# Two-layer spectral convolution on one core: x loaded first, bytes and loads moved at three stage starts, the first mixing weights on another engine

## The chip, the cores and the metric

One core of one Trainium2 chip. The metric is the device time of one execution in microseconds; a profiled execution also gives a span, from the first to the last instruction. Engines: TensorE (PE, with its weight loads shown as PEld), VectorE (DVE), ScalarE (ACT), GpSimd (POOL) and SyncE (SP). SP computes nothing here; its queue (SPq) issues nearly all transfers, one after the other.

## The reference, cut to what matters

The input x is 16 images of 16 channels of 256 x 256 values, float32. Layer 0 normalises x by groups of two channels, applies a circular 3 x 3 convolution (written with FFTs) and adds x. Layer 1 normalises again, goes to the frequency domain, mixes channels at each frequency with a matrix built from poles and residues, goes back, and adds a transient term:

```
x = x + conv3x3(gn(x), weight)
alpha = fft2(gn(x))
A = 1/(i*w1 - pole1);  Bm = 1/(i*w2 - pole2)
S = einsum('ikpq,oikp,xikq->oxik', residue, A, Bm)
r1 = einsum('biox,oxik->bkox', alpha, S)
r2 = einsum('bikpq,ikpq->bkpq', einsum(alpha, A, Bm), residue)
x = x + real(ifft2(r1)) + real(sum of r2 * exp(pole1*ty) * exp(pole2*tx)) / (Nx*Ny)
```

## The kernel before

The work is one program in four stages, one after the other. Each stage opens its own pools in the on-chip memory, over the bytes of the stage before. A tile that lands on bytes of an earlier tile waits until that tile's last readers and writers are done; the kernel inserts these waits by itself. Inside the stages the order on each engine is the order in which the code records it (`manual_schedule`), and every engine and queue works in order. So an instruction that waits holds up all that stand behind it on its engine. Transfers use eight DMA semaphores in turn: the issue of a transfer waits until the one eight places earlier has landed.

**Stage 1, convolution (lines 100 to 651).** An image is held as two halves of 128 partitions x 18 x 258, loaded by `load_x` (line 111). Per image `x_stats` takes 16 `bn_stats` of VectorE (line 156), eight from each half, aggregates them (line 164), spreads the groups' sums over the partitions with small matmuls (line 168), and folds the scale into the convolution's weights (`conv_weights`). `sum_taps` (line 136) reads the weights' tile `wband` and is run between the eighth and the ninth `bn_stats` of image 0. Then `conv(g)` gives TensorE its matmuls (line 239); ScalarE evicts them to a tile `vt` with sums (lines 256, 264; four buffers), VectorE adds and subtracts the mirrored rows (lines 221, 222), and the two results, `vsum` and `vt`, are stored to the scratch `vD` (line 282). For the first image nothing is there to overlap with: the convolution starts when its statistics are done. Between the convolution's steps, tables for the later stages are made from the poles: exponentials, the table `cD` of residues over frequencies, and others, which need the reciprocal step sizes `rd` (lines 74 to 76).

Before stage 1, `const` (line 47) loads `cols`, `kmask` and `fold2`, then `step` (the first two values of ty and tx, from which `rd` is made) and a part of `tabE` and `tabO`: seven loads ahead of x.

**Stage 2, transform (lines 654 to 851).** 64 units, each of one channel and four images. `load_v` (line 684) reads `vD` into a tile `s` with four transfers, two units ahead; `fold` (line 692) makes `vq` from it on VectorE and GpSimd; `lines` (lines 720, 728, 736) transforms along y and scales on ScalarE; `columns` (lines 748 to 783) transforms along x into `spec`, and after the fourth unit of a channel `spec` (4 MB) is stored to `aD` (line 848). `spec` alternates between two places, one for even and one for odd channels. `first_slots` (line 792) multiplies by `sgn`, a column of -1 and a column of 1, set by two memsets at the start of the stage (lines 680, 681). `sgn` is a tile of 4 KB per partition, of which 8 bytes are used; it also keeps the two places of `spec` apart. The first three units' loads are issued by GpSimd (line 815).

**Stage 3, mixing (lines 855 to 1109).** `ct` (4 MB) is read from `cD` (line 885). `weights(g)` (line 904) builds one group's factors `v` on VectorE and multiplies them by four column masks, `m4`, into the tile `w` of 2048 columns on GpSimd (line 933). `sums` (line 962) multiplies `ct` and `w` on TensorE into the mixing matrices, which are evicted to `sg`; `mix` (line 1028) applies them to `abd`, the spectra loaded from `aD` (line 1014) into tiles that GpSimd first clears (line 977). The first `sums` need `weights(0)`, and after eight rounds `weights(32)`. `ct` lies over the bytes of the even `spec` and, with its last 96 bytes, over the first bytes of `sgn`'s tile.

**Stage 4, inverse transform (lines 1112 to 1306).** Back along x and y, the transient term added, the residual from `vD` added, and the result stored. The change does not touch it.

Of the kernel before, what the change touches and what calls it, by code (L numbers as in the profile page):

```python
# [9 lines left out]
FP = mybir.dt.float32  # L10
AF = mybir.ActivationFunctionType
ALU = mybir.AluOpType
# [5 lines left out]
C = 16  # L18
N = 256
P = 128  # L20
# [4 lines left out]
def conv_then_laplace_kernel(ctx: ExitStack, tc: tile.TileContext, a: dict, out: bass.AP):  # L25
# [15 lines left out]
    nc = tc.nc  # L41
    x = a["x"]
# [1 line left out]
    cp = ctx.enter_context(tc.tile_pool(name="const", bufs=1))  # L44
    dp = ctx.enter_context(tc.tile_pool(name="scratch", bufs=1, space=DRAM))

    def const(name, shape, src=None):
        t = cp.tile(shape, FP, name=name, tag=name)
        nc.sync.dma_start(out=t, in_=a[name] if src is None else src)
        return t  # L50

    cols = const("cols", [P, 24])
# [15 lines left out]
        nc.vector.tensor_scalar(o, k, d, 2.0 * PI, ALU.mult, ALU.mult)  # L68

    step = cp.tile([P, 2, 2], FP, name="step", tag="step")  # L70
    nc.sync.dma_start(out=step[:, 0], in_=a["ty"][:, 0:2].to_broadcast([P, 2]))
    nc.sync.dma_start(out=step[:, 1], in_=a["tx"][:, 0:2].to_broadcast([P, 2]))
    rd = cp.tile([P, 2], FP, name="rd", tag="rd")
    nc.vector.tensor_tensor(rd, step[:, :, 1], step[:, :, 0], ALU.subtract)
    nc.vector.tensor_scalar(rd, rd, float(N), None, ALU.mult)
    nc.vector.reciprocal(rd, rd)

    ptab = ExitStack()
    tp = ptab.enter_context(tc.tile_pool(name="tables", bufs=1))
# [4 lines left out]
    tabO = tp.tile([P, C + 1, P], FP, name="tabO", tag="tabO")  # L84
    hB = tp.tile([P, 2, C, P], FP, name="hB", tag="hB")
    coef = [tp.tile([P, C, 4, 4, 2], FP, name=f"coef{j}", tag=f"coef{j}") for j in range(2)]
    nc.sync.dma_start(out=tabE[:, 0], in_=a["trig"][:, 0])
    nc.sync.dma_start(out=tabO[:, C], in_=a["trig"][:, 1])

# [8 lines left out]
    p1 = ExitStack()  # L98
# [9 lines left out]
    psu = p1.enter_context(tc.tile_pool(name="p_setup", bufs=1, space=PSUM))  # L108
    p1.enter_context(tc.manual_schedule())

    def load_x(b, h):
        t = xp.tile([P, 18, N + 2], FP, name="xt", tag="xt")
        nc.sync.dma_start(out=t, in_=x[b][:, 16 * h : 16 * h + 18])
        return t

    halves = {0: [load_x(0, 0)]}

    def load1(name, shape, pool=wp):
        t = pool.tile(shape, FP, name=name, tag=name)
# [4 lines left out]
    imask = load1("imask", [P, 2, 3, 32], tp)  # L124
    g128 = load1("g128", [P, P], tp)
    m16 = load1("m16", [P, C], tp)
    halves[0].append(load_x(0, 1))
    halves[1] = [load_x(1, h) for h in range(2)]
    nc.sync.dma_start(out=jmat, in_=a["jmat"])
    ones = tp.tile([P, P], FP, name="ones", tag="ones")  # L130
# [487 lines left out]
    for j, (_, piece) in enumerate(x_stats(0)):  # L618
        if j == 8:
            sum_taps()  # L620
        piece()

    at_step = {}
# [37 lines left out]
    def pool(stage, name, bufs=1, **kw):  # L661
        return stage.enter_context(tc.tile_pool(name=name, bufs=bufs, reuse_waits="tile", **kw))
# [3 lines left out]
    fp = pool(p1, "fold_2", 2)  # L666
    lp = pool(p1, "lines", 2)
    a0 = pool(p1, "spec_even")
    kp = pool(p1, "b_const")
    a1 = pool(p1, "spec_odd")  # L670
    kpp = pool(p1, "sines", 3)
    prp = pool(p1, "prod", 2)
    pa = pool(p1, "p_y", 3, space=PSUM)
    px = pool(p1, "p_x", 4, space=PSUM)
    pd = pool(p1, "p_d", space=PSUM)
    p1.enter_context(tc.manual_schedule())


    sgn = kp.tile([P, 1024], FP, name="sgn", tag="sgn")[:, 0:2]
    nc.vector.memset(sgn[:, 0:1], -1.0)  # L680
    nc.vector.memset(sgn[:, 1:2], 1.0)
    m, n = cols[:, 16:17], cols[:, 17:18]

    def load_v(i, b0, eng=nc.sync):
# [127 lines left out]

    units = [(i, b0) for i in range(C) for b0 in range(0, B, 4)]

    loaded = {u: load_v(*units[u], nc.gpsimd) for u in range(3)}
    vq = fold(*units[0], loaded.pop(0))
    nc.vector.bn_aggr(ms[:, B - 1], vst[:, B - 1])
    rest = v_stats(B - 4, B, lambda: pa.tile([P, 512], FP, name="ps_y", tag="ps_y"))
    last = None
# [84 lines left out]
    def weights(g):  # L904

        shape = [P, 32, 4]
        u = up.tile([P, 4, 32, 4], FP, name="u", tag="u")
        w, den, e, f = (u[:, j] for j in range(4))  # L910
        pr2, pre, pim = (prU[:, j].unsqueeze(2).to_broadcast(shape) for j in range(3))
        nc.vector.tensor_tensor(
            w,
            omg[:, g].unsqueeze(1).to_broadcast(shape),
            pims.unsqueeze(2).to_broadcast(shape),
            ALU.subtract,
        )
        nc.vector.tensor_tensor(den, w, w, ALU.mult)
        nc.vector.tensor_tensor(den, den, pr2, ALU.add)
# [10 lines left out]
        nc.vector.tensor_scalar(v[:, :, 0, 1], v[:, :, 1, 0], -1.0, None, ALU.mult)  # L930
        wt = wp.tile([P, 4, 8, 2, 32], FP, name="w", tag="w")
        full = [P, 64, 4, 8]
        nc.gpsimd.tensor_tensor(  # L933
            wt.rearrange("p a k o (i m) -> p (a k o) i m", i=4),
            v.rearrange("p a o r s -> p (a o) (r s)").unsqueeze(2).to_broadcast(full),
            m4.unsqueeze(1).unsqueeze(3).to_broadcast(full),
            ALU.mult,
        )
        return wt
# [516 lines left out]
```

## Time and profile before

Median of three runs 2817.53 us (2812.63 to 2821.07); the profiled execution has a span of 2806.7 us. Stages by the first and last matmuls of each, from the busy times by stretch:

| stretch, us | what | PE busy | DVE | ACT | POOL | PE clock | DMA share |
|---|---|---|---|---|---|---|---|
| 0 to 29.5 | ahead of the convolution | 1.70 | 13.89 | 1.49 | 0.19 | 1.00 | 0.87 |
| 29.5 to 643.0 | convolution | 526.45 | 518.62 | 435.03 | 279.73 | 0.95 | 0.74 |
| 643.0 to 655.8 | between | 0.03 | 5.75 | 2.96 | 0.00 | 0.52 | 0.61 |
| 655.8 to 1276.6 | transform | 617.85 | 520.81 | 371.65 | 220.00 | 0.99 | 0.58 |
| 1276.6 to 1300.7 | between | 0.01 | 16.82 | 0.58 | 14.16 | 0.61 | 0.85 |
| 1300.7 to 2010.0 | mixing | 705.02 | 340.95 | 378.11 | 122.44 | 0.99 | 0.67 |
| 2010.0 to 2806.7 | inverse transform | 765.72 | 511.49 | 332.94 | 439.03 | 0.99 | 0.86 |

Busy is in us; the clock is the share of full speed that TensorE was granted, and the DMA share is the mean busy share of the core's 16 DMA engines. A profile line of the timeline gives start, duration, engine, source line, operation, output and inputs; a bracket at its end is the idle time of that engine before it and what seems to have ended it. The releaser is inferred, and where several things are waited for only one is named.

### The profile page before, as it was taken

What the parts mean: (1) busy time and instruction counts of PE and PEld (TensorE: products, weight loads), DVE (VectorE), ACT (ScalarE), POOL (GpSimd) and SP (SyncE); (2) the same over time, 40 slices, a digit from 0 to 9 for tenths busy, and PEclk for the clock granted to TensorE, in tenths of its full rate; (3) what the DMA queues carried; (4) which work ended last, traced back from release to release, by engine and by line L of the source; (5) the groups of instructions that cost most, each with busy time, mean ns of one, the idle gap of its engine ahead of it and who ended that gap; (6) DMA issues with size and microseconds to landing.
All of it is one profiled execution on the core that took longest, in us unless ns stands there. A gap on an engine that the chain in (4) does not pass through costs nothing.

```text
span 2806.7 us, 93073 instructions
## 1 busy us (share of the span) xinstructions
PE 2616.8 (93%) x39600; PEld 1958.4 (70%) x39600; DVE 1928.3 (69%) x3562; ACT 1522.8 (54%) x3090; POOL 1075.6 (38%) x997
## 2 busy tenths in 40 slices
PE   5878988797999999996999999999989999999998
PEld 2434444355777777774888888888778888888887
DVE  6888998867888888885454444444346666666666
ACT  3767777664666666663455555555434444444443
POOL 1543466513333333334111111111165656565653
PEclk9999999898999999998999999999999999999999
DMA  7776887655665656654766666676688999989995
GB/s 270 255 248 247 286 285 267 230 185 166 229 229 208 213 203 240 227 193 162 200 189 194 190 192 192 194 195 193 198 274 284 289 284 288 283 286 286 288 284 179
DMA packets 479375, 652.82 MB, mean 233 GB/s; under 512 B 51352, under 2 KB 457880, under 8 KB 465008
## 3 DMA queue, kind: packets, MB, share of 16 engines
q1 hardware_dynamic: 477248, 637.56, 70.5%
q8 instruction: 312, 5.11, 0.7%
q0 software_dynamic: 1568, 5.11, 0.6%
q10 hardware_dynamic: 144, 4.19, 0.3%
q14 instruction: 103, 0.84, 0.1%
HBM read 367.22 MB, written 279.50 MB: 230 GB/s over the span
## 4 chain that ended last, share of the span: by engine, by line
PE 61%; DVE 14%; DMA 12%; POOL 4%; issue 4%; SPq 2%; ACT 1%; DVEq 0%; POOLq 0%; ACTq 0%
PE ps_mix L1028 16%; PE ps_s L962 9%; PE ps_y L720 8%; PE ps_y L728 8%; DMA yk<-yD 6%; PE ps_x L763 4%; PE ps_conv L239 4%; PE ps_p L1212 3%; DVE r L1245 3%; PE ps_f L1236 3%; PE ps_f L1237 3%; DMA out_y<-ol 3%; DVE xst L156 2%; DMA xt<-in_x 2%; SPq L1159 2%
## 5 line engine op out<-in xcount | busy, mean ns | idle before, releaser
L1028 PEld LDWEIGHTS ps_mix<-abd,sg 128*64 128x64 f32 x8192 | 449.1, 138 | 61.5 <-ACT sg L1085 48.9
L1028 PE MATMUL ps_mix<-abd,sg 128*64 128x128 f32 x8192 | 480.0, 276 | 9.5 <-ACT yt L1090 9.5
L239 PE MATMUL ps_conv<-xt,wc 32*32 32x512 f32 x12288 | 463.3, 618 | 27.2 <-issue 24.8
L1176 POOL TENSOR_TENSOR u<-yk 128x512 f32<-128x512 f32 (+1 forms) x268 | 346.0, 1322 | 317.7 <-PE ps_p L1212 210.3
L736 ACT ACTIVATE t<-ps_y,vmr 128x384 f32<-128x384 f32 x512 | 297.2, 581 | 166.7 <-PE ps_y L728 166.6
L239 PEld LDWEIGHTS ps_conv<-xt,wc 32*32 32x32 f32 x12288 | 231.4, 105 | 214.4 <-issue 139.4
L933 POOL TENSOR_TENSOR w<-v,mcol 128x2048 f32<-128x2048 f32 x33 | 119.3, 3616 | 575.3 <-DVE v L930 546.9
L1090 DVE COPY yt<-ps_mix 128x512 f32<-128x512 f32 x128 | 88.5, 691 | 360.7 <-PE ps_mix L1028 238.5
L720 PE MATMUL ps_y<-tabE,vq 128*128 128x256 f32 x1024 | 313.5, 388 | 15.0 <-DVE vq L709 13.4
L728 PE MATMUL ps_y<-tabO,vq 128*128 128x256 f32 x1024 | 306.1, 381 | 0.0
L1236 PE MATMUL ps_f<-pt,inv 128*128 128x256 f32 x1008 | 300.4, 380 | 0.0
L1090 ACT COPY yt<-ps_mix 128x512 f32<-128x512 f32 x384 | 220.5, 586 | 146.5 <-PE ps_mix L1028 88.4
L1237 PE MATMUL ps_f<-hs,ey 128*128 128x256 f32 x1008 | 299.8, 379 | 0.0
L1212 PEld LDWEIGHTS ps_p<-inv,u 128*128 128x128 f32 x2048 | 266.0, 193 | 45.0 <-issue 25.1
L1212 PE MATMUL ps_p<-inv,u 128*128 128x128 f32 x2048 | 279.4, 280 | 8.4 <-POOL u L1180 8.3
L962 PE MATMUL ps_s<-ct,w 64*32 64x256 f32 x8448 | 261.2, 382 | 24.4 <-POOL abd L977 24.1
L1240 DVE TENSOR_TENSOR r<-ps_f,q 128x256 f32<-128x256 f32 x256 | 106.9, 418 | 251.5 <-ACT q L1239 251.5
L1085 ACT COPY sg<-ps_s 128x512 f32<-128x512 f32 x248 | 159.7, 645 | 190.7 <-PE ps_s L962 190.6
L720 PEld LDWEIGHTS ps_y<-tabE,vq 128*128 128x128 f32 x1024 | 189.7, 191 | 91.5 <-ACT q L776 50.3
L256 ACT ACTIVATE vt<-ps_conv,xq 128x512 f32<-128x512 f32 x256 | 167.0, 680 | 155.9 <-PE ps_conv L239 140.7
L1239 ACT COPY q<-ps_f 128x256 f32<-128x256 f32 x256 | 95.4, 372 | 287.6 <-PE ps_f L1237 284.4
L1214 ACT COPY pt<-ps_p 128x512 f32<-128x512 f32 x256 | 150.1, 586 | 133.3 <-PE ps_p L1212 117.9
(238 smaller groups left out, 4170.4 us busy)
## 6 DMA issues: line engine op xcount, KB each, us to landing
xt<-in_x SPq DMA_DIRECT2D x32, 2322.0 KB, 10.8
abd<-aD SPq DMA_DIRECT2D x512, 128.0 KB, 2.9
yD<-yt SPq DMA_DIRECT2D x512, 128.0 KB, 2.6
vl<-vD SPq DMA_DIRECT2D x256, 256.0 KB, 4.1
out_y<-ol SPq DMA_DIRECT2D x128, 512.0 KB, 9.2
s<-vD SPq DMA_DIRECT2D x244, 256.0 KB, 6.7
aD<-spec SPq DMA_DIRECT2D x15, 4096.0 KB, 12.5
yk<-yD SPq DMA_DIRECT2D x60, 1024.0 KB, 8.5
```

The lines of the kernel that those rows point to most:

```text
L239: nc.tensor.matmul(acc[r][32 * c : 32 * c + 32], lhsT=ready[b][0][rows, phase, tap], rhs=halves[b][u // 2][rows, q : q + 5 : 4, 2 - tap : ...
L256: nc.scalar.activation(vt[:, r % 2], acc[r], AF.Identity, bias=ready[b][1], **by_sums)
L720: nc.tensor.matmul(ps[:, 0:N], lhsT=vf[:, xo, 0, j], rhs=tabE[:, 0 : i + 2 : i + 1], start=True, stop=False, skip_group_check=True,)
L728: nc.tensor.matmul(ps[:, P : P + N], lhsT=vf[:, xo, 1, j], rhs=tabO[:, i : C + 1 : C - i], start=False, stop=True, skip_group_check=True,)
L736: nc.scalar.activation(t[:, xo, j].rearrange("p l n -> p (l n)"), ps[:, 0:384], AF.Copy, scale=vmr[:, 0, b0 + j, i : i + 1],)
L962: nc.tensor.matmul(ps[odd][32 * iq : 32 * iq + 32, ro], lhsT=w[rows, iq, kk, ro], rhs=ct[rows, iq, kk], start=True, stop=True,)
L1028: nc.tensor.matmul(ps[64 * t : 64 * t + 64, j], lhsT=sg[:, f : f + 2].rearrange("p f m -> p (f m)"), rhs=abd[jq][:, :, 2 * t + cc, 2 * jj ...
L1090: (nc.vector.tensor_copy if m == 3 else nc.scalar.copy)(o, src)
L1176: nc.gpsimd.tensor_tensor(u[:, :, j].rearrange("p b (c n) -> p c b n", c=8), in0, in1, o)
L1212: nc.tensor.matmul(ps[:, at], lhsT=u[:, n], rhs=tab, start=True, stop=True)
L1236: nc.tensor.matmul(ps[:, e], lhsT=tab, rhs=pt[:, e], start=True, stop=False)
L1237: nc.tensor.matmul(ps[:, e], lhsT=ey[:, e], rhs=hs, start=False, stop=True)
```

## The change

Four edits:

1. **x first.** The constants, `step` and the two table parts are no longer loaded where they are declared: they are put on a list and loaded by `load_consts()` after x and the convolution's tables. Image 0's first half is loaded in three parts (rows 0 to 5, 5 to 9, 9 to 18), each of which releases the `bn_stats` that read it, and its second half directly after. The three operations on `rd` move from the top of VectorE's queue to behind the last `bn_stats` of image 0.
2. **Stage 2's constant and second loads.** `sgn` becomes a tile of two columns in a pool of its own at the end of the stage's memory; an unused tile of 4 KB stays between the two places of `spec`. The two memsets move behind the first `fold`. Units 1 and 2 are loaded by SP's queue; unit 0 stays with GpSimd. In the built program unit 1's four issues stand between the stores of the last two groups, and unit 2's behind the last.
3. **The residues' table.** With `sgn` gone from there, `ct` overlaps only the even `spec` (and the unused tile). In the built program its issue now stands ahead of the three small loads of stage 3's constants, no longer behind them, and waits for the store of channel 14's `spec`.
4. **First mixing weights.** For group 0 alone the product with the masks is split by mask column: three quarters on ScalarE, one on GpSimd.

```diff
-    def const(name, shape, src=None):
+    def load_consts():
+        for t, src in later_loads:
+            nc.sync.dma_start(out=t, in_=src)
+    later_loads = []
+    def const(name, shape):
         t = cp.tile(shape, FP, name=name, tag=name)
-        nc.sync.dma_start(out=t, in_=a[name] if src is None else src)
+        later_loads.append((t, a[name]))
...
-    nc.vector.tensor_tensor(rd, step[:, :, 1], step[:, :, 0], ALU.subtract)
-    nc.vector.tensor_scalar(rd, rd, float(N), None, ALU.mult)
-    nc.vector.reciprocal(rd, rd)
+    def inverse_steps():
+        nc.vector.tensor_tensor(rd, step[:, :, 1], step[:, :, 0], ALU.subtract)
+        nc.vector.tensor_scalar(rd, rd, float(N), None, ALU.mult)
+        nc.vector.reciprocal(rd, rd)
...
-    def load_x(b, h):
+    def load_x(b, h, parts=(0, 18)):
         t = xp.tile([P, 18, N + 2], FP, name="xt", tag="xt")
-        nc.sync.dma_start(out=t, in_=x[b][:, 16 * h : 16 * h + 18])
+        for i, j in zip(parts, parts[1:]):
+            nc.sync.dma_start(out=t[:, i:j], in_=x[b][:, 16 * h + i : 16 * h + j])
...
-    halves = {0: [load_x(0, 0)]}
+    halves = {0: [load_x(0, 0, (0, 5, 9, 18)), load_x(0, 1)]}
...
-    halves[0].append(load_x(0, 1))
+    load_consts()
...
+        if j == 16:
+            inverse_steps()
...
-    kp = pool(p1, "b_const")
+    kp = pool(p1, "between")
...
+    bp = pool(p1, "b_const")
...
-    sgn = kp.tile([P, 1024], FP, name="sgn", tag="sgn")[:, 0:2]
-    nc.vector.memset(sgn[:, 0:1], -1.0)
-    nc.vector.memset(sgn[:, 1:2], 1.0)
+    kp.tile([P, 1024], FP, name="between", tag="between")
+    sgn = bp.tile([P, 2], FP, name="sgn", tag="sgn")
...
-    loaded = {u: load_v(*units[u], nc.gpsimd) for u in range(3)}
+    loaded = {u: load_v(*units[u], nc.sync if u else nc.gpsimd) for u in range(3)}
     vq = fold(*units[0], loaded.pop(0))
+    nc.vector.memset(sgn[:, 0:1], -1.0)
+    nc.vector.memset(sgn[:, 1:2], 1.0)
...
         wt = wp.tile([P, 4, 8, 2, 32], FP, name="w", tag="w")
+        if g == 0:
+            v2 = v.rearrange("p a o r s -> p (a o) (r s)")
+            w4 = wt.rearrange("p a k o (i m) -> p (a k o) i m", i=4)
+            for i in range(3):
+                nc.scalar.activation(w4[:, :, i], v2, AF.Copy, scale=m4[:, i : i + 1])
+            nc.gpsimd.tensor_scalar(w4[:, :, 3], v2, m4[:, 3:4], None, ALU.mult)
+            return wt
```

More of the change, by code (lines that the diff above doesn't have):

```diff
@@ L70, in conv_then_laplace_kernel @@
     step = cp.tile([P, 2, 2], FP, name="step", tag="step")
-    nc.sync.dma_start(out=step[:, 0], in_=a["ty"][:, 0:2].to_broadcast([P, 2]))
-    nc.sync.dma_start(out=step[:, 1], in_=a["tx"][:, 0:2].to_broadcast([P, 2]))
     rd = cp.tile([P, 2], FP, name="rd", tag="rd")
-    nc.vector.tensor_tensor(rd, step[:, :, 1], step[:, :, 0], ALU.subtract)
-    nc.vector.tensor_scalar(rd, rd, float(N), None, ALU.mult)
-    nc.vector.reciprocal(rd, rd)
+    later_loads.append((step[:, 0], a["ty"][:, 0:2].to_broadcast([P, 2])))
+    later_loads.append((step[:, 1], a["tx"][:, 0:2].to_broadcast([P, 2])))
+    def inverse_steps():
+        nc.vector.tensor_tensor(rd, step[:, :, 1], step[:, :, 0], ALU.subtract)
+        nc.vector.tensor_scalar(rd, rd, float(N), None, ALU.mult)
+        nc.vector.reciprocal(rd, rd)
     ptab = ExitStack()
@@ L86, in conv_then_laplace_kernel @@
     coef = [tp.tile([P, C, 4, 4, 2], FP, name=f"coef{j}", tag=f"coef{j}") for j in range(2)]
-    nc.sync.dma_start(out=tabE[:, 0], in_=a["trig"][:, 0])
-    nc.sync.dma_start(out=tabO[:, C], in_=a["trig"][:, 1])
+    later_loads.append((tabE[:, 0], a["trig"][:, 0]))
+    later_loads.append((tabO[:, C], a["trig"][:, 1]))
     p1 = ExitStack()
```

## The prediction

> **What bounds the kernel now.** I read first the busy times of each engine by stage. TensorE works nearly without a gap inside the four stages (617.85 of 620.8 us in the transform, 705.02 of 709.3 in the mixing); it stands still ahead of the first stage (29.5 us) and between stages. All edits lie at three of those gaps, so I read the timeline there.
>
> First gap, timeline of the start (start us, duration us, engine, line, operation; in brackets the idle time before it and its releaser):
>
> ```profile
> 4.02 0.43 SPq L113 DMA_DIRECT2D xt<-in_x  x1
> ...
> 6.95 1.48 SPq L113 DMA_DIRECT2D xt<-in_x  x3
> ...
> 13.17 4.85 DVE L156 BATCH_NORM_STATS2 xst<-xt 128x6 f32<-128x512 f32 x8 [7.29 <-DMA xt<-in_x]
> ...
> 19.53 4.85 DVE L156 BATCH_NORM_STATS2 xst<-xt 128x6 f32<-128x512 f32 x8 [0.54 <-DMA xt<-in_x]
> 24.42 0.59 DVE L164 BATCH_NORM_AGGREGATE xq<-xst 128x2 f32<-128x96 f32 x1
> ...
> 29.49 10.32 PE L239 MATMUL ps_conv<-xt,wc 32*32 32x512 f32 x176
> ```
>
> The first half of image 0 is issued behind seven small loads; the second half lands at 19.53 and sets everything up to the convolution at 29.49.
>
> Second gap, convolution to transform:
>
> ```profile
> 639.88 0.88 SPq L282 DMA_DIRECT2D vD<-vt  x2
> ...
> 645.44 0.69 ACT L256 ACTIVATE vt<-ps_conv,xq 128x512 f32<-128x512 f32 x1 [3.51 <-DMA vD<-vt]
> ...
> 648.18 1.22 DVE L222 TENSOR_TENSOR vt<-vt 128x1024 f32<-128x1024 f32 x1
> ...
> 652.46 0.06 DVE L680 MEMSET sgn<- 128x1 f32 x1 [3.05 <-DMA vD<-vt]
> ...
> 652.56 1.14 DVE L698 SCALAR_TENSOR_TENSOR vf<-s,vmr 128x128 f32<-128x128 f32 x4
> ```
>
> Two waits on a store of vt: the eviction waits 3.51 us for its buffer, then a memset of two columns waits 3.05 us for bytes that vt held, with the whole first fold queued behind it. TensorE has been done since 642.3 and restarts at 655.8.
>
> Third gap, transform to mixing:
>
> ```profile
> 1279.68 0.33 SPq L885 DMA_DIRECT2D ct<-cD  x1
> ...
> 1286.45 0.23 DVE L930 TENSOR_SCALAR v<-v 128x128 f32<-128x128 f32 x1
> ...
> 1286.91 3.75 POOL L933 TENSOR_TENSOR w<-v,mcol 128x2048 f32<-128x2048 f32 x1 [3.79 <-DVE u L912]
> ...
> 1287.24 3.57 DVE L919 TENSOR_TENSOR u<-u,prU 128x128 f32<-128x128 f32 x1
> ...
> 1300.70 18.44 PE L962 MATMUL ps_s<-ct,w 64*32 64x256 f32 x512 [24.09 <-POOL abd L977]
> ```
>
> The view names a memset of abd as releaser, but this matmul reads only ct and w. The first w is done at 1290.66; the list of DMA issues gives ct its landing:
>
> ```profile
> ct<-cD SPq DMA_DIRECT2D x1, 4096.0 KB, 20.9
> ```
>
> 1279.68 + 20.9 = 1300.6: ct ends the wait, TensorE having stopped at 1276.6. ct was issued so late because its last bytes overlap sgn's tile, which GpSimd reads to 1279.65.
>
> **What the Trainium skill says.** "DMA: Bandwidth & Descriptors", Queues, rings and completion order: the DMA engines take turns between the queues that have work, and consume one queue in order. The trace agrees: ct and the last aD store, 4 MB each on two queues, need 20.9 us together, where an aD store alone has a median of 12.5. "SBUF — State Buffer", Who interferes with whom: GpSimd shares a port pair with VectorE operations of two SBUF inputs, as an exclusive lock; ScalarE waits on nobody. Agrees: line 919 took 3.57 us beside the GpSimd product, and 0.29 at its median. "TensorE: Matmul & The Clock Gate", Part 1: an idle TensorE falls to half rate and needs some microseconds of work to recover. Agrees: the clock is 0.50 from 645 to 655 and from 1285 to 1300. The remaining gaps stay far above its 3.4 us, so the cold restart is paid as now.
>
> **The change, part by part.**
>
> *Start.* Issues are 0.47 us apart, so x's three parts go out at 0.73, 1.20 and 1.67, the second half at 2.14. How long until data flows: a two-column load took 2.6 us issue to landing, which I take as latency. How fast: between 13.17 and 19.53 the second half's 2.38 MB came at 0.37 MB/us while the next loads were in flight; the window's rate reaches 0.43. So 4.76 MB from 0.73+2.6 need 11.1 to 12.8 us: landing at 14.4 to 16.1; I take 14.8. The eight reductions of the first half end by about 11.5 and cost nothing. But wband now stands behind x and sum_taps, in front of the second eight, needs it: say 0.3 us more, and its 1.05 us (0.46+0.18+0.35 and gaps), formerly hidden in the wait for x, now lie on the path, as do the three operations on rd (0.6 us) ahead of the aggregate. End of the statistics: 14.8+0.3+1.05+4.85+0.6 = 21.6, against 24.4: **2.8 us**, from 1.5 to 3.2. The added waits: the build hands out eight DMA semaphores in turn, so an issue waits for the one eight places earlier. Image 1's halves stand at places 16 and 17 and wait for m16, which lies behind x: issue near 17 instead of 7.4, landing near 25 and 30.5. They are needed at 29.73-2.8 = 26.9 and 4.85 later, 31.8: 1 to 2 us of slack. The steps' two loads go out when the second half has landed and are needed 5 us later; the other moved constants are first used after 37 us: no cost.
>
> *Second gap.* GpSimd issued 12 loads of s from 630.16 on, 3 MB that competed with the stores. Now only unit 0 goes there; units 1 and 2 stand in SP's queue behind the stores of the last groups but one and the last. The store issued at 639.88 to 640.76 then lands about 2.4 us after its issue (the shortest landing in this window is 2.2) instead of 645.4: near 643.3, not before the last matmuls at 642.3. That gives 2 us, between 0 and 2.9. The memset moves behind the first fold and to bytes last used long ago: 3.1 us, from the end of line 222 (649.4) to 652.56. Sum **5.0 us**, from 3.1 to 6. What queues behind: unit 1, issued near 641 to 643, lands by 648 and is needed near 654; unit 2, issued after the last stores (near 649), lands by 656 and is needed near 664. Neither is on the path.
>
> *Third gap.* With sgn elsewhere, ct overlaps only the even spec, which is free when the store issued at 1244.37 has landed: about 1257. No loads of s are left then, so ct lands near 1270, hidden by the transform. The first weights become next: v is ready at 1286.7, then three ScalarE products of 512 columns. The nearest rows are 0.63 us (line 500, 128x512 from SBUF) and 0.72 (line 264): 3 x 0.66 and gaps = 2.1 us. The GpSimd quarter runs beside them (0.69 at line 487, up to 2.63 under contention). TensorE starts at 1288.8, at worst 1290, instead of 1300.7: **11.8 us**, from 10.5 to 12. Behind it: VectorE's line 919 loses only some 0.7 us instead of 3.3, so the second product starts near 1290.3 and ends near 1294.2; it is needed after eight rounds, 9.7 us after the start, 1298.5. The memsets of abd end near 1298 and 1301, the aD store, now alone, lands near 1292.5, abd0 is loaded by 1301 and first used at 1322.9-11.8 = 1311. So the shift holds.
>
> Sum: 2.8+5.0+11.8 = 19.6 us; 2817.5-19.6 = **2798**. The gaps follow one another, so the gains add.
>
> **The rivals.**
> *The start and the stores give nothing*: image 1 comes too late by as much as image 0 gained, or the convolution stage (TensorE busy 526 of 613 us, so paced by several engines) swallows it, and the vt store is as slow as before. For it: the slack of 1 to 2 us. Against: that stage runs on dependent work from the first statistics on. 3.1+11.8 = 14.9: 2803.
> *A new wait takes ct's place*: slow strided products on ScalarE and a blocked GpSimd quarter, or abd0. For it: no row has this access pattern. Against: 10 us of slack on abd0. A gain of 4 there: 2.8+5.0+4 = 11.8, 2806.
> *Slower*: the later loads of x put every following image out of step. SP is one queue in order, and six statistics wait 21.6 us for x between 60 and 600 us, so the stage is sensitive. 1.5 us for each of 15 images cost 22.5: 2817.5+22.5-19.6 = 2820; a little more per image is slower beyond doubt. Against: these loads wait for the convolution, not for the start.
>
> **How the numbers follow.** Forecast 75%, the rivals 11, 9 and 5. The timed runs of before spread from 2812.6 to 2821.1, so 4 us of noise go on either side. Best sum 3.2+6+12 = 21.2, so 2796, less noise and something unforeseen: low 2788. High 2809 takes in the first two rivals. Faster by over 0.3% (under 2809.1): 0.90; within: 0.07; slower: 0.03.
>
> **What would show it.** After: the second eight reductions start near 16.5 and the convolution near 26.7; the first fold follows the last subtraction (line 222) with no gap, the eviction's wait under 2 us; ct is issued about 12 us after the store of the last even spec; the first mixing matmul starts about 12 us after the last transform matmul, not 24, released by ScalarE. I am wrong if the span from the first convolution to its last matmul grows by more than 2 us, or if the first mix waits for abd.

## The result, and the profile after

The kernel before takes 2817.68 us in the median of four runs (2812.63 to 2821.07), the changed one 2791.86 us (2782.28 to 2796.88). The ratio is 0.9911, with a 95% interval of 0.9883 to 0.9939: some 25 us faster. A second series of the same kernel, described last among the experiments, gave 0.9909 (0.9891 to 0.9927). The prediction was 2798, with a range of 2788 to 2809.

The first gap in the timeline of the changed kernel (start us, duration us, engine, line, operation; in brackets the idle time before it and what ended it):

```profile
0.73 2.04 SPq L123 DMA_DIRECT2D xt<-in_x  x4
...
8.98 2.48 DVE L166 BATCH_NORM_STATS2 xst<-xt 128x6 f32<-128x512 f32 x4 [1.51 <-DMA xt<-in_x]
...
14.86 0.47 DVE L147 TENSOR_REDUCE wsum<-wband 128x32 f32<-128x192 f32 x1 [3.40 <-DMA wband<-in_wband]
...
15.84 4.84 DVE L166 BATCH_NORM_STATS2 xst<-xt 128x6 f32<-128x512 f32 x8
...
21.06 0.57 DVE L174 BATCH_NORM_AGGREGATE xq<-xst 128x2 f32<-128x96 f32 x1
...
26.11 11.22 PE L249 MATMUL ps_conv<-xt,wc 32*32 32x512 f32 x176
...
26.36 9.59 DVE L166 BATCH_NORM_STATS2 xst<-xt 128x6 f32<-128x512 f32 x16
```

The first eight reductions now run while x is still coming. In the trace each transfer makes sixteen updates of a semaphore; where a landing is given below without a line, it is the time of the last of them. So x's second half lands at 14.55 and `wband`, which is issued behind it, at 14.83. `wband` releases the sum of the taps, and the second eight reductions follow it. The convolution starts 3.38 us earlier (29.49 to 26.11). The sixteen reductions of image 1 run in one piece: its halves land at 25.00 and 30.56 and are first read at 26.36 and 31.11, with 1.4 and 0.6 us to spare.

The second gap in the same view:

```profile
638.17 0.69 ACT L266 ACTIVATE vt<-ps_conv,xq 128x512 f32<-128x512 f32 x1 [0.41 <-PE ps_conv L249]
...
640.91 1.23 DVE L232 TENSOR_TENSOR vt<-vt 128x1024 f32<-128x1024 f32 x1
642.06 1.13 DVE L710 SCALAR_TENSOR_TENSOR vf<-s,vmr 128x128 f32<-128x128 f32 x4
...
645.27 1.19 PE L732 MATMUL ps_y<-tabE,vq 128*128 128x256 f32 x2 [7.11 <-DVE vq L721]
...
646.20 0.06 DVE L829 MEMSET sgn<- 128x1 f32 x1
```

Neither of the two waits on a store of vt is left. The eviction waits 0.41 us, and for TensorE, not 3.51 us for a store; the first fold follows the last subtraction directly. The last convolution matmul ends at 633.39 + 4.76 = 638.15, so the gap is 7.12 us; before it was 655.77 - 642.32 = 13.45.

The third gap:

```profile
1245.33 0.33 SPq L899 DMA_DIRECT2D ct<-cD  x1
...
1275.96 0.23 DVE L944 TENSOR_SCALAR v<-v 128x128 f32<-128x128 f32 x1
...
1276.23 1.95 ACT L951 ACTIVATE w<-v,mcol 128x512 f32<-128x512 f32 x3 [9.42 <-DVE v L944]
...
1276.46 1.69 POOL L952 TENSOR_SCALAR w<-v,mcol 128x512 f32<-128x512 f32 x1 [3.83 <-DVE u L926]
1276.75 0.67 DVE L933 TENSOR_TENSOR u<-u,prU 128x128 f32<-128x128 f32 x1
...
1278.27 16.82 PE L984 MATMUL ps_s<-ct,w 64*32 64x256 f32 x465 [12.16 <-POOL w L952]
```

`ct` is issued at 1245, no longer 3 us after the transform's last matmul, and lands at 1258.20, 20 us before it is read. Now the weights end the wait: ScalarE's third product ends at 1276.23 + 1.95 = 1278.18, GpSimd's quarter at 1278.15. The gap falls from 24.09 to 12.16 us.

The table puts the profiles side by side. It is worked out from first and last matmuls: "start" is the first convolution matmul, "rest" everything from the first matmul on `ct` to the end of the span. The runs from the third row on are the experiments below.

| profile | start | convolution | gap 2 | transform | gap 3 | rest | span |
|---|---|---|---|---|---|---|---|
| before | 29.49 | 612.8 | 13.45 | 620.84 | 24.09 | 1506.0 | 2806.7 |
| changed | 26.11 | 612.0 | 7.12 | 620.84 | 12.16 | 1502.2 | 2780.5 |
| e1, start alone | 26.35 | 614.7 | 12.49 | 620.85 | 25.35 | 1510.0 | 2809.7 |
| e2, loads alone | 29.16 | 610.9 | 11.35 | 620.86 | 24.00 | 1501.8 | 2798.0 |
| e3, bytes alone | 29.66 | 615.2 | 9.82 | 620.78 | 14.12 | 1502.0 | 2791.5 |
| e4, weights alone | 29.28 | 616.7 | 13.59 | 620.84 | 24.15 | 1511.7 | 2816.3 |
| a1, changed less weights | 26.31 | 613.4 | 7.12 | 620.85 | 13.96 | 1500.6 | 2782.2 |
| a2, changed, old bytes | 26.35 | 612.4 | 7.11 | 620.86 | 25.38 | 1502.8 | 2794.9 |
| a3, x in six parts | 23.28 | 615.6 | 7.11 | 620.85 | 12.16 | 1509.5 | 2788.5 |
| a4, weights early | 26.12 | 614.1 | 7.12 | 623.94 | 6.37 | 1508.5 | 2786.2 |
| a6, image 1 early | 22.50 | 615.3 | 7.11 | 620.84 | 12.16 | 1509.2 | 2787.1 |
| a7, a4 mended | 26.18 | 616.3 | 7.12 | 620.84 | 3.20 | 1514.6 | 2788.3 |
| a8, a6 and a7 | 22.47 | 619.8 | 7.12 | 620.84 | 3.20 | 1513.2 | 2786.6 |
| changed, again | 26.13 | 613.5 | 7.11 | 620.84 | 12.16 | 1509.3 | 2789.0 |

Start, gaps and transform of one program repeat to some tenths of a microsecond; the convolution and the rest vary by several whatever is edited. So an edit of a gap is read from its gap; from the times only where there are many runs. A difference of times given below with a ratio is worked out from the ratio, which sets a kernel against the runs of the kernel before in its own series; the plain medians can differ from it by 2 us.

### The profile page after: what moved, and what is told of

Same layout as the page of the kernel before. It is cut to its first block, busy times and chain, and to the rows that moved or that the text cites. A ratio compares the mean times of both kernels' runs of the same rounds, so it can differ in the third digit from the quotient of the medians.

```text
span 2780.5 us, 93064 instructions
## 1 busy us (share of the span) xinstructions
PE 2614.0 (94%) x39600; PEld 1956.3 (70%) x39600; DVE 1927.2 (69%) x3562; ACT 1524.6 (55%) x3093; POOL 1069.9 (38%) x989
## 4 chain that ended last, share of the span: by engine, by line
PE 64%; DVE 13%; DMA 11%; POOL 4%; issue 4%; ACT 2%; SPq 2%; DVEq 0%; ACTq 0%; POOLq 0%
PE ps_mix L1050 16%; PE ps_s L984 9%; PE ps_y L732 8%; PE ps_y L740 8%; DMA yk<-yD 5%; PE ps_conv L249 5%; PE ps_x L775 4%; PE ps_p L1234 4%; PE ps_f L1258 3%; PE ps_f L1259 3%; DMA out_y<-ol 3%; DVE r L1267 2%; DVE xst L166 2%; PE psd L760 1%; SPq L1181 1%
## 5 line engine op out<-in xcount | busy, mean ns | idle before, releaser
L984 PE MATMUL ps_s<-ct,w 64*32 64x256 f32 x8448 | 261.2, 382 | 13.1 <-POOL w L952 12.2
```

Source lines behind the costliest of these rows:

```text
L984: nc.tensor.matmul(ps[odd][32 * iq : 32 * iq + 32, ro], lhsT=w[rows, iq, kk, ro], rhs=ct[rows, iq, kk], start=True, stop=True,)
```

## The experiments

My theory is that of the prediction: each edit shortens its own gap, the gaps follow one another, and the gains add. The main rivals: the convolution stage swallows an earlier start; the loads of `s` had nothing to do with the slow store; GpSimd, which the trace named at the third gap, sets its end and not `ct`. The kernels e1 to e4 each add one part to the kernel before, a1 and a2 take one away from the changed kernel, a3 to a8 go further along the same lines.

### e1: the start alone

```diff
-    halves = {0: [load_x(0, 0)]}
+    halves = {0: [load_x(0, 0, (0, 5, 9, 18)), load_x(0, 1)]}
...
-    halves[0].append(load_x(0, 1))
+    load_consts()
...
+        if j == 16:
+            inverse_steps()
```

> The kernel before with the first part alone: x's two halves first, the constants and the steps behind them. My theory (the gaps follow one another, each gain is kept): the first convolution starts at about 26.1 us instead of 29.5, its last matmul moves by the same 3.4 us from 642.3 to about 638.9, the two later gaps stay at 13.4 and 24.1 us, and the time falls by 3.4 us to about 2814. Rival (the convolution stage swallows it, being paced by several engines and by the loads of x): the start moves, the last convolution matmul stays within 1 us of 642.3, the time stays at 2817.5.

Measured: 2810.58 us, ratio 0.9986 (0.9973 to 0.9999): 3.9 us less, with 0.3 to 7.6 in the interval. The convolution starts at 26.35, and its last matmul ends at 641.00, where 638.9 was expected. The four profiles with the old start (before, e2, e3, e4) end the convolution anywhere between 640.0 and 646.0, so that one profile decides nothing; averages say more. Seven profiles have this edit and no other at the start (the changed kernel's two, e1, a1, a2, a4, a7). On average their convolution starts 3.2 us earlier than in the four, the statistics of image 6 are aggregated 3.0 us earlier (at 242.9, not 245.9), and the last matmul ends 3.3 us earlier (640.0, not 643.3; single profiles scatter about these means by 1.4 and 2.7). The stage keeps the early start to its end, and the rival falls.

At the third gap this trace, unlike that of before, names the right releaser, in its timeline:

```profile
1299.69 10.70 PE L974 MATMUL ps_s<-ct,w 64*32 64x256 f32 x265 [25.35 <-DMA ct<-cD]
```

### e2: units 1 and 2 on SyncE's queue alone

```diff
-    loaded = {u: load_v(*units[u], nc.gpsimd) for u in range(3)}
+    loaded = {u: load_v(*units[u], nc.sync if u else nc.gpsimd) for u in range(3)}
```

> The kernel before with one edit alone: the loads of s for units 1 and 2 stand in SyncE's queue, only unit 0 stays on GpSimd's. My theory (12 early loads slow the store that the last eviction waits for): the eviction's wait of 3.51 us falls under 1 us, the memset of sgn still waits about 3 us for the last store, and the gap of TensorE between the convolution and the transform falls from 13.4 to about 10.3 us; time about 2814.5. Rival (the store is as slow without them): gap 13.4, time 2817.5. A second rival (units 1 and 2 now come late): the gap shrinks and the transform grows beyond 620.8 us.

Its timeline at the second gap:

```profile
640.05 0.69 ACT L256 ACTIVATE vt<-ps_conv,xq 128x512 f32<-128x512 f32 x1 [0.41 <-PE ps_conv L239]
...
648.07 0.06 DVE L680 MEMSET sgn<- 128x1 f32 x1 [4.05 <-DMA vD<-vt]
...
651.38 1.19 PE L720 MATMUL ps_y<-tabE,vq 128*128 128x256 f32 x2 [11.35 <-DVE vq L709]
```

The eviction's wait is gone, as expected: the early loads of `s` had slowed the store it waited for. But the memset now waits 4.05 us instead of 3.05 for the last store, which is in flight together with loads of units 1 and 2 and lands 3.2 us after its issue, where it took 2.4 before. The gap falls by 2.1 us, not by 3. The transform stays at 620.86, so the later loads hold nobody up. The time is 2805.36, ratio 0.9978 (0.9968 to 0.9989): 6.2 us less, with 3.1 to 9.0 in the interval. That is more than the gap shows, and no view tells where the excess lies: in its profile the convolution is 2 us shorter, but the kernel does nothing else than the one before until 627 us.

### e3: sgn's bytes alone, its memsets where they were

```diff
-    sgn = kp.tile([P, 1024], FP, name="sgn", tag="sgn")[:, 0:2]
+    kp.tile([P, 1024], FP, name="between", tag="between")
+    sgn = bp.tile([P, 2], FP, name="sgn", tag="sgn")
     nc.vector.memset(sgn[:, 0:1], -1.0)
```

> The kernel before with one edit alone: sgn gets bytes of its own at the end, and its two memsets stay ahead of the first fold. My theory (the bytes cause both waits: the memset waits for vt's store, and the load of ct waits for the last read of sgn): the gap ahead of the transform falls by 3.1 us to about 10.3; ct is issued some 12 us after the store of channel 14's spectrum, the wait ahead of the mixing is ended by the first weights of GpSimd, and that gap falls from 24.1 to about 14.0 us. Time 2817.5 - 3.1 - 10.1 = about 2804. Rival (GpSimd's products and the memset of abd, which the trace names as releaser, set the end of the third gap, not ct): the third gap stays at 24, time 2814.

Its timeline:

```profile
647.55 0.69 ACT L256 ACTIVATE vt<-ps_conv,xq 128x512 f32<-128x512 f32 x1 [3.11 <-DMA vD<-vt]
...
654.65 1.19 PE L722 MATMUL ps_y<-tabE,vq 128*128 128x256 f32 x2 [9.82 <-DVE vq L711]
...
1254.64 0.33 SPq L887 DMA_DIRECT2D ct<-cD  x1
...
1285.74 3.75 POOL L935 TENSOR_TENSOR w<-v,mcol 128x2048 f32<-128x2048 f32 x1 [3.80 <-DVE u L914]
1286.08 3.57 DVE L921 TENSOR_TENSOR u<-u,prU 128x128 f32<-128x128 f32 x1
...
1289.55 18.82 PE L964 MATMUL ps_s<-ct,w 64*32 64x256 f32 x512 [14.12 <-POOL w L935]
```

This one edit acts at both gaps. At the second the memset no longer waits, while the eviction still does (3.11 us), and the gap falls by 3.6 us. At the third, `ct` is issued 11.4 us after the store of channel 14's `spec` (1243.20), and the gap falls from 24.09 to 14.12, now ended by the weights. The time is 2798.36, ratio 0.9953 (0.9937 to 0.9970): 13.2 us less (8 to 18), as worked out. GpSimd's chain, with the memset of `abd` that the trace of before had named, is as it was, and TensorE starts 10 us earlier: the rival falls.

### e4: the first weights alone

```diff
+        if g == 0:
+            for i in range(3):
+                nc.scalar.activation(w4[:, :, i], v2, AF.Copy, scale=m4[:, i : i + 1])
+            nc.gpsimd.tensor_scalar(w4[:, :, 3], v2, m4[:, 3:4], None, ALU.mult)
+            return wt
```

> The kernel before with one edit alone: the first mixing weights as three products on ScalarE and a quarter on GpSimd. My theory (ct ends the wait at 1300.6, the weights lie ready ten us earlier): weights ready about 2 us earlier, third gap still 24.1 us, time 2817.5. Rival (GpSimd's chain of two products and the memset, as the trace names it, sets the end): the second product starts some 3 us earlier, third gap 21, time about 2814.5.

Its timeline:

```profile
1283.50 0.33 SPq L885 DMA_DIRECT2D ct<-cD  x1
1290.54 1.95 ACT L937 ACTIVATE w<-v,mcol 128x512 f32<-128x512 f32 x3 [9.41 <-DVE v L930]
...
1304.57 1.96 PE L970 MATMUL ps_s<-ct,w 64*32 64x256 f32 x32 [24.15 <-DMA ct<-cD]
```

The weights are ready at 1292.5 and wait 12 us for `ct`. The gap is 24.15, the ratio 1.0000 (0.9985 to 1.0015). Alone this part is worth nothing at the gap, and the time shows nothing either.

### a1: the changed kernel without ScalarE's weights

```diff
-        if g == 0:
-            for i in range(3):
-                nc.scalar.activation(w4[:, :, i], v2, AF.Copy, scale=m4[:, i : i + 1])
-            nc.gpsimd.tensor_scalar(w4[:, :, 3], v2, m4[:, 3:4], None, ALU.mult)
-            return wt
```

> The changed kernel without its last part: the first mixing weights come from one GpSimd product of 2048 elements again. My theory (with ct early the weights end the wait): third gap 12.2 + 2 = about 14.1 us, as in the run that moved only sgn's bytes (14.12); time 2 us above the changed kernel, about 2794. Rival (something else ends the wait, so that ScalarE's products are worth nothing): third gap 12.2, same time as the changed kernel. Second rival (the GpSimd product is slowed to some 7 us by the shared port): gap 17, 5 us above.

Its timeline:

```profile
1277.95 3.60 POOL L947 TENSOR_TENSOR w<-v,mcol 128x2048 f32<-128x2048 f32 x1 [3.79 <-DVE u L926]
...
1281.60 3.67 PE L976 MATMUL ps_s<-ct,w 64*32 64x256 f32 x64 [13.96 <-POOL w L947]
```

With `ct` early the weights end the wait, and the part is worth 13.96 - 12.16 = 1.8 us at the gap. The second rival does not show: GpSimd's product took 3.60 us, not 7. The time, 2787.45 (ratio 0.9914, 0.9890 to 0.9938), cannot tell 1.8 us from nothing.

### a2: the changed kernel with sgn back on its old bytes

```diff
-    kp.tile([P, 1024], FP, name="between", tag="between")
-    sgn = bp.tile([P, 2], FP, name="sgn", tag="sgn")
+    sgn = kp.tile([P, 1024], FP, name="sgn", tag="sgn")[:, 0:2]
```

> The changed kernel with sgn back on its old bytes, its memsets left behind the first fold. My theory (the bytes alone decide when ct is loaded, the place of the memset only the second gap): second gap as in the changed kernel, about 7.1 us; ct issued after the last read of sgn, near 1269, together with the last aD store, so that the third gap is 24 us and is ended by ct; time 12 us above the changed kernel, about 2804. Rival (the memset still waits for a store of vt and holds the fold of unit 1): the transform grows by 1 to 3 us too. Rival (ct's time of issue does not matter): third gap 12.

Its timeline:

```profile
646.83 0.06 DVE L827 MEMSET sgn<- 128x1 f32 x1
...
1269.83 0.33 SPq L897 DMA_DIRECT2D ct<-cD  x1
...
1292.13 2.39 PE L982 MATMUL ps_s<-ct,w 64*32 64x256 f32 x40 [25.38 <-DMA ct<-cD]
```

The second gap stays at 7.11: behind the fold, the memset finds the store of vt landed (at 646.44), and old bytes cost it nothing. The third gap is back, at 25.38 us. The time is 2802.31, ratio 0.9960 (0.9941 to 0.9980), 14 us above the 0.9911 of the changed kernel. So at the second gap either the memset's place or its bytes would have done; at the third it is the bytes.

### a3 and a6: further along at the start

In the changed kernel VectorE still waits 3.40 us for `wband`, with the second eight reductions behind it. a3 issues `wband` between x's halves and cuts the second half into the same three parts.

```diff
-    halves = {0: [load_x(0, 0, (0, 5, 9, 18)), load_x(0, 1)]}
+    halves = {0: [load_x(0, 0, (0, 5, 9, 18))]}
     wband = load1("wband", [P, 2, 3, 32], tp)
+    halves[0].append(load_x(0, 1, (0, 5, 9, 18)))
```

> The changed kernel with one thing more at the start: wband is loaded between x's two halves, and the second half comes in the same three parts as the first. My theory (data flows at a fixed rate, so the reductions can run as parts land, and the sum of taps no longer stands behind all of x): of the second eight reductions half are done when the last part lands near 14.6, the statistics end about 17.3 instead of 20.7, and the convolution starts near 22.8 instead of 26.1; time 3 us below the changed kernel, about 2789. Rival (image 1's halves, issued later, now hold up its reductions): start earlier, but a wait of 1 to 3 us for x in the reductions of image 1, and no gain in time.

The convolution starts at 23.28, 2.8 us earlier, and the timeline shows the rival:

```profile
24.89 4.85 DVE L167 BATCH_NORM_STATS2 xst<-xt 128x6 f32<-128x512 f32 x8 [1.29 <-DMA xt<-in_x]
30.65 4.85 DVE L167 BATCH_NORM_STATS2 xst<-xt 128x6 f32<-128x512 f32 x8 [0.90 <-DMA xt<-in_x]
35.53 0.59 DVE L175 BATCH_NORM_AGGREGATE xq<-xst 128x2 f32<-128x96 f32 x1
```

Image 1's statistics wait for both of its halves and end at 35.53, 0.45 us before the 35.98 of the changed kernel. The time is 2789.07, ratio 0.9912 (0.9891 to 0.9933): no gain shows, though the interval could hide one of 3 us. a6 therefore also loads image 1 ahead of the constants.

```diff
-    load_consts()
     halves[1] = [load_x(1, h) for h in range(2)]
+    load_consts()
...
-        if j == 16:
-            inverse_steps()
...
+        inverse_steps()
         nc.vector.tensor_scalar(top, rd, 2.0 * PI * P, None, ALU.mult)
```

> As the run that loaded x's second half in parts (a3), and image 1's two halves are moved ahead of the later constants, with the three operations on rd moved to just before their first use. In a3 the convolution started at 23.28 us, but the statistics of image 1 waited 1.29 and 0.90 us for its halves, and ended only 0.45 us earlier than in the changed kernel. My theory (those halves, issued at 16.3 and 19.7 behind the constants, took the gain): they are issued near 10, the reductions of image 1 run without a wait from about 23 and end near 32.7 instead of 35.98, and the time falls by 3 us against the changed kernel, to about 2787. Rival (the convolution stage swallows an earlier start, being paced by the later images): statistics of image 1 earlier, the last convolution matmul not, no gain.

Its timeline:

```profile
22.75 9.59 DVE L167 BATCH_NORM_STATS2 xst<-xt 128x6 f32<-128x512 f32 x16
32.37 0.59 DVE L175 BATCH_NORM_AGGREGATE xq<-xst 128x2 f32<-128x96 f32 x1
...
61.00 2.48 DVE L167 BATCH_NORM_STATS2 xst<-xt 128x6 f32<-128x512 f32 x4 [4.16 <-DMA xt<-in_x]
...
72.67 0.59 DVE L175 BATCH_NORM_AGGREGATE xq<-xst 128x2 f32<-128x96 f32 x1
```

Image 1 no longer waits, and is 3.6 us ahead of the changed kernel. Image 2 then waits 4.16 us for its second half, against 2.55 in the changed kernel; that half is issued at 48.47 (49.72 there), behind stores in SyncE's queue. Its statistics end 1.4 us ahead (72.67 against 74.06). So each early start meets the next load of x. On average the three profiles with a start near 23 (a3, a6, a8) are 1.3 us ahead of the seven with a start near 26 at image 2 (72.7 against 74.0) and no longer ahead at image 6 (243.2 against 242.9); their last convolution matmul ends at 639.7, that of the seven at 640.0. The first 3 us at the start were kept, the next 3 are gone by image 6: in the profiles the rival holds. The time is nevertheless the lowest of all: 2781.56, ratio 0.9876 (0.9860 to 0.9892), 9 to 10 us below the two series of the changed kernel, though the intervals would allow about 3. The start does not explain it, and the profile, whose span of 2787.1 belongs to the slowest of its runs, shows nothing else; it stays open.

### a4 and a7: further along at the third gap

The remaining 12 us are the end of the transform on VectorE and the preparation of the weights, which hangs on nothing in the transform. a4 prepares `v` for the first group during units 4 to 7, in fifteen operations on VectorE, from copies of the constants in the unused tile, and puts all four products on ScalarE.

```diff
-    kp.tile([P, 1024], FP, name="between", tag="between")
+    kp.tile([P, 24], FP, name="between", tag="between")
+    first_consts = load_weight_consts(kp)
+    first_weights = poles(0, first_consts, u0, v0)
...
+        if 4 <= u < 12:
+            next(first_weights, None)
```

> The changed kernel with the first mixing weights prepared during the transform: their constants are loaded into the padding between the two spectra, VectorE's twenty operations on them are spread over units 4 to 7, and all four products stand on ScalarE behind the last copy of q. My theory (ct is there by 1270, and only the weights hold the mixing back): third gap falls from 12.2 to about 3.5 us, the time by 8 to about 2783. Rivals: the second set of weights (wanted eight rounds later) becomes the wait, which gives back 1 to 4 us inside the first sums; or the loads of abd hold the first mix, which gives back all but some 2 us; or VectorE has no room in the transform, which then grows by up to 5 us.

Its timeline:

```profile
647.21 0.34 SPq L90 DMA_DIRECT2D p2k<-in_pole_k  x1
...
651.48 0.35 DVE L760 SCALAR_TENSOR_TENSOR vf<-s,vmr 128x128 f32<-128x128 f32 x1 [2.93 <-DMA s<-vD]
...
1275.07 2.56 ACT L962 ACTIVATE w<-o,mcol 128x512 f32<-128x512 f32 x4 [3.06 <-DVE spec L853]
...
1277.68 4.33 PE L997 MATMUL ps_s<-ct,w 64*32 64x256 f32 x66 [6.37 <-ACT w L962]
1282.56 4.75 PE L997 MATMUL ps_s<-ct,w 64*32 64x256 f32 x152 [0.55 <-DVE other L1028]
```

The third gap falls to 6.37, by 5.8 us, and nearly all of that is given back. The new constants' loads wait in SyncE's queue until vt's store has left their bytes, with `s` of units 1 and 2 behind them: the folds wait up to 2.93 us and the transform grows by 3.1. The issue of the last `aD` store stands on ScalarE's queue, waits there for the last write of `spec`, and holds the products 3.06 us. And the first sums up to the first mix take 25.0 us, where the changed kernel's two profiles have 22.8 and 21.8: VectorE's work on the second weights stands in front of its copies, and TensorE waits 0.55 us for one of them. The rest of that growth is not accounted for. The time is 2790.45, ratio 0.9921 (0.9901 to 0.9940). a7 mends the three.

```diff
+        if u == 3:
+            fetch_weight_consts(first_consts)
+        if 8 <= u < 16:
+            next(first_weights, None)
...
-                (nc.sync if i + 1 < C else nc.scalar).dma_start(
+                (nc.sync if i + 1 < C else nc.gpsimd).dma_start(
...
-                    copy = (nc.scalar.copy, nc.vector.tensor_copy)[odd]
+                    copy = (nc.scalar.copy, nc.vector.tensor_copy)[odd and 8 * h + kk > 2]
```

> As the run that prepared the first mixing weights in the transform (a4), mended in the three places where its trace lost the gain: the constants' loads are issued after unit 6's and not ahead of units 1 and 2 (the transform grew 3.1 us, folds waited for s), the last aD store goes to GpSimd's queue instead of ScalarE's, ahead of the four products (they waited for the last copy of spec), and ScalarE makes all copies of the first three rounds while VectorE works on the second weights (the first sums grew 2.2 us). My theory: transform 620.8 again, third gap near 3.3 us instead of 12.2, first sums near 23; time 8 to 9 us below the changed kernel, about 2783. Rival (the second weights or abd's loads set the first mix, whatever the first sums do): the gap shrinks, but the first sums grow by as much, and the time stays near 2791.

(The steps moved on to units 8 to 11.) Its timeline:

```profile
1271.04 2.56 ACT L966 ACTIVATE w<-o,mcol 128x512 f32<-128x512 f32 x4
...
1273.65 5.36 PE L1001 MATMUL ps_s<-ct,w 64*32 64x256 f32 x162 [3.21 <-ACT w L966]
1281.73 7.14 PE L1001 MATMUL ps_s<-ct,w 64*32 64x256 f32 x179 [2.71 <-DVE other L1032]
```

The transform is back at 620.84 and the gap at 3.20. The first sums still take 25.1 us, since VectorE's copies come too late at 1281.7; gap and sums together fall from 34.96 to 28.35 us (by 6.6; by 5.6 against the second profile of the changed kernel). The time is 2788.98, ratio 0.9901 (0.9887 to 0.9914), 2 to 3 us below the changed kernel where 8 to 9 were expected. The intervals do not tell 2.5 us from 6.6, nor from nothing. The mixing and the inverse stage of its profile are longer by 10 us than in the first profile of the changed kernel and by 2 than in the second. Whether something there gives part of the gain back stays open.

### a8: a6 and a7 together

> Both of the above in one kernel. My theory (the gaps follow one another, gains add): 3 + 8.5 us below the changed kernel, about 2780, start near 23.1, second gap 7.1, third gap 3.3. Rival (what one gains is lost in the other stages): no faster than the better of the two alone.

Start, gaps and transform are those of its two parts (22.47, 7.12, 620.84, 3.20). The time is 2784.45, ratio 0.9880 (0.9863 to 0.9897), no faster than a6 alone, as the rival has it; of the 8.5 us that a7's part was to add, the intervals would allow some 5. a6 has the lowest median of all kernels here.

### The changed kernel again

> The changed kernel once more, nothing edited, to tell what of a difference between two profiles is the edit and what differs between two executions of one program. My theory (the gaps and the transform are set by fixed chains, the convolution stage and the inverse stage by many interleaved queues): start 26.1 to 26.4, second gap 7.1, transform 620.8, third gap 12.2, each within 0.3 us; convolution stage anywhere between 612 and 616, inverse stage between 766 and 776; time 19 to 26 us below the kernel before, ratio 0.991 to 0.993. Rival (the 3.8 us that the pair of profiles showed beyond the three gaps are part of the change): convolution stage within 0.5 us of 612.0, everything after the third gap within 1 us of 1502.2 (22.8 + 711.6 + 767.8), ratio near 0.9905.

Measured: 2790.82 against 2814.61, ratio 0.9909 (0.9891 to 0.9927). Start, gaps and transform repeat to 0.02 us. The convolution takes 613.5 instead of 612.0 and the rest 1509.3 instead of 1502.2. Against the profile of before, the first profile of the changed kernel was shorter by 0.8 us in the convolution and 3.8 in the rest, and this one is longer by 0.7 and 3.3. Such differences therefore say nothing of the change.

## Why the prediction was right

The three gaps of the first pair add up to 3.38 + 6.33 + 11.93 = 21.6 us, where 19.6 was predicted; the time fell by 25.8 and, in the second series, by 23.8 us, and both intervals hold 21.6.

Each part was set too low, and two of the three lie above their own ranges (1.5 to 3.2 at the start, 3.1 to 6 at the second gap); their sum is above the best sum of 21.2. What brought the time into its range is the margin for noise and the unforeseen.

*Start, 2.8 predicted, 3.38 measured.* The chain was the right one, and each link came out a little shorter. The second half of x landed at 14.55, not at 14.8, and `wband` 0.28 us behind it, as the 0.3 has it. The sum of the taps took 1.0 us, and the second eight reductions started at 15.84 (the sum gives 16.15; the 16.5 among the signs does not agree with it). The three operations on `rd` cost 0.4 us between the last reduction and the aggregate, and not 0.6. The halves of image 1 landed when they were expected, near 25 and 30.5, but were needed sooner: the slack was 1.4 and 0.6 us, not 1 to 2, and a3 uses it up.

*Second gap, 5.0 predicted, 6.33 measured.* The wait of the memset was sized rightly. Mis-sized is the term "that gives 2 us, between 0 and 2.9", because the prediction took the wrong store. By the semaphores on which it waits, the eviction at 645.44 does not need the store issued at 639.88, which landed only at 648.63, but the one before it:

```profile
633.86 1.31 SPq L282 DMA_DIRECT2D vD<-vt  x2
```

The second of these two transfers was issued at 634.31 and landed at 645.34, 11.0 us later. In the four profiles with all twelve early loads on GpSimd's queue (before, e1, e3, e4) it took 10.3 to 11.9 us, in the ten others 5.6 to 7.4. Without those loads it is in memory ahead of the last matmul: the eviction waits for no store at all (0.41 us, for TensorE), and the whole distance from the last matmul to the eviction, 645.44 - 642.32 = 3.1 us, falls away. That the early loads of `s` slow the store was right, and e2 shows it, in which they are the only edit and the wait falls to 0.41 us. That the estimate came near with another store is luck.

*Third gap, 11.8 predicted, 11.93 measured.* Both waits stood one behind the other, as the prediction had it: `ct` (e3: 10.0 us), and behind it the weights (a1: 1.8 us; alone, e4: nothing). VectorE lost 0.67 - 0.29 us beside the quarter on GpSimd, less than assumed. The releaser named is GpSimd's quarter and not ScalarE; they end 0.03 us apart, and the quarter took 1.69 us, within the bounds that were set.

*The shift behind the third gap held.* No wait for `abd0` came up; the first mix starts 1301.08 - 1278.27 = 22.8 us after the first sums, before 22.2. The cold restart was paid as before: TensorE's granted clock is 0.50 for 7.2 us from the first transform matmul on (8.3 before) and for 5.7 us from the first sums on (5.1 before).

*The rivals.* None of the three came about in the changed kernel. The worry about the loads of x was a real one, though: a3 and a6 run into it as soon as the start moves another 3 us.

The Trainium skill, *"DMA: Bandwidth & Descriptors", Queues, rings and completion order,* says that the DMA engines take turns among the queues that have work. The third gap rests on it, and this case agrees: beside the last `aD` store `ct` took 20.8 to 22.2 us (before, e1, e2, e4, a2), and 12.3 to 13.1 in the nine profiles in which it had landed before that store was issued. That the engines also consume one queue in order carried nothing here: what held back `s` in a4 were loads not yet issued, which is the order of SyncE's instructions.

The Trainium skill, *"SBUF — State Buffer", Who interferes with whom,* says that VectorE operations of two SBUF inputs share a port pair with GpSimd's reads, and that who issues first holds it for the whole instruction. Beside the product of 2048 elements this fits: in e3 the VectorE operation took 3.57 us and ended 0.16 us after the product. Beside the quarter it fits less well: the operation took 0.67 us and ended at 1277.42, while the quarter is recorded until 1278.15. How long the quarter held the ports is not shown.

What stays open: the time fell by 2 to 4 us more than the gaps did, in both series of the changed kernel (within the intervals), and by more than the gap in e2 too (6.2 us against 2.1, and 3.1 at the least). No profile shows where.

## What to carry to other kernels

When the trace names one releaser for an instruction that waits for several things, list what the instruction reads and when each was ready: here a memset on another engine was named, and a 4 MB load that waited for a few shared bytes was the cause. The same goes for a wait on a store: several stores of one tile are in flight, and the one that was issued last need not be the one that is waited for. Waits stand one behind the other, so that a part that is worth nothing alone (e4) is worth its 1.8 us once the wait in front of it is gone; price each edit with the others in place. And an earlier start is only kept as far as the later loads let it through: here the first 3 us of it were kept to the end of the stage, and the next 3 were gone by image 6.

## What the runs showed of the hardware that was not expected

- One program's start, gaps and transform repeated to 0.02 us between two executions, while its convolution stage differed by 1.4 us and everything after the third gap by 7.1 us.
- `ct`, 4 MB beside the last `aD` store, took 20.8 to 20.9 us in before, e2 and e4, and 22.1 to 22.2 in e1 and a2, which have the early start in common; what that has to do with it 1240 us later is not known. Apart from each other, `ct` took 12.3 to 13.1 us, and the store on ScalarE's queue 11.9 to 12.0 instead of 22.9 to 23.1.
- A transfer's issue on ScalarE's queue holds the arithmetic behind it until the transfer's own input is ready: 3.06 us in a4, gone in a7 with the issue on GpSimd.
- GpSimd's one-input product of 128x512 took 1.69 us, ScalarE's 0.71 (1.95 for three, one after the other).
- A store of 256 KB took 10.3 to 11.9 us beside twelve loads of the same size issued by GpSimd, and 5.6 to 7.4 where only four of these stood there.
